# Four graph layers on one core: attention of a graph starts half a graph earlier, and the dilation holds two edge buffers instead of three

## The chip, the core and the metric

The kernel runs on one core of a Trainium2 chip. The metric is the device time in microseconds of one execution. A core has five engines with a queue each: PE (matmul), DVE (vector), ACT (activation), POOL (GpSimd) and SP, which here only issues DMAs. Each queue works strictly in its order; engines wait for each other and for DMAs by semaphores. POOL issues DMAs too: those that change the element type, and the loads of adjacency.

## What is computed

There are 16 graphs of 1024 nodes with 128 features, and four layers, each followed by a residual sum and a layer normalization:

```
x0: v, q, k = relu(x W + b); h = masked clip(q k^T); x = LN(x + softmax(h) v)
x1: p = x (W1 - W2) + b; q = x W2
    x = LN(x + max over neighbours j of relu(p_i + q_j))
x2: agg = A^T x;  x = LN(x + mask * (relu(((1+eps) x + agg) W1 + b1) W2 + b2))
x3: A' = dilate(A): for n = 0..1023 in turn: of row n, every (ceil(num/2))-th neighbour is
    removed when num > 10 (every one when 1 < num <= 10), and column n with it
    three SAGE layers on A' with normalized rows and batch norms over all graphs, a linear layer
    x = LN(x + linear)
```

The dilation depends on the adjacency alone, so it runs beside layers 0 to 2. It is sequential: what row n removes changes the rows after it.

## The kernel before

**The piece loop.** Layer 1's maximum over neighbours is done by table. The 1024 possible neighbours of a graph are cut into NP = 86 pieces of 12, each of two groups of 6. `tables_of` (its maxima are L492) builds, for sets of pieces, the maximum of q over each of the 64 subsets of a group; `table` and `low_part` turn two pieces of a set on PE and split them into a high and a low part (L848 to L858). `count` (L835, L836) makes on PE and ACT a one-hot `hot` that says which subset each node has as neighbours. `look_up` (L867) multiplies table by hot into PSUM (`pg`), and DVE takes the maximum into `best` (L932; L926 for the first piece). A piece is worked in two halves of 512 nodes; `slot(s)` writes down the work of piece s out of 16 x 86 = 1376. Two `pg` buffers exist.

**Order.** In the piece loop the order of PE, ACT, DVE and POOL is what the program writes down (`manual_schedule`); SP's order is set by the framework. Beside the pieces run generators called streams: `scores(b)` and `attend(b)` (layer 0 and the two products of layer 1 for graph b), `tables_of(b)`, and `rest(b)` (end of layer 1 and layer 2). A stream yields `ask(engine, cost, ...)` and goes on when its engine's account in `room` is positive, a delay in pieces has passed, and an event such as `("q", b)` has happened. The accounts are refilled at each half piece out of ROOM (L792; the new values are in the change). In graph b's 86 pieces the kernel also works on the attention of b+1 and on `rest(b-1)`.

**Row buffers and adjacency.** `X[b]` (three buffers) holds the node rows of a graph; SP loads it at the first piece of graph b-1. `An[b]` (two buffers) holds the adjacency rows of a graph. POOL loads them once for `scores` and once more for `rest` (L757).

**The dilation.** `dilation()` is a generator of its own that goes on when its due time in pieces has come. It works 32 rows at a time, all 16 graphs side by side: K = 32 blocks of about 43 pieces. Block k:

- DVE adds up counts and writes `rest` (L661).
- POOL runs 31 steps, one for each row but the last of the block (L675 to L685). Each step is ten small instructions that depend on each other. The program writes a step down every 1.03 pieces, and between the steps it writes down `behind`, the removal of block k-1's edges from all columns (`remove`: PE turns E and ranks the edges, DVE marks the removed), and then `prepare(k+1)`.
- `hit` goes to DRAM and comes back in another layout on SP (L692, L695).
- DVE turns it (`hit_T`, L709) and cuts E; POOL works out the block's numbers (L713 on).

`load(k)` allocates and fetches block k's edges `E` (four POOL DMAs, L518; three buffers), fetches `gone_T` (SP, L523), clears `counts` (POOL, L529) and allocates V. It is called for block k+1 at the start of block k, ahead of the first step:

```
work = [behind]
if k + 1 < K:
    following = load(k + 1)
    work.append((cost, False) for cost in prepare(k + 1, *following))
```

After the piece loop a last phase computes layer 3 (its aggregations are L1096), about 1.1 ms.

Of the kernel before, what the change touches and what calls it, by code (L numbers as in the profile page):

```python
# [29 lines left out]
F32 = mybir.dt.float32  # L30
# [17 lines left out]
NP = -(-N // PS)  # L48
TG = 12
R, G = 32, 4  # L50
GONE = 1
# [4 lines left out]
LOWEST = -(2.0**100)  # L56
MAGIC = 2.0**23
CLAMP_HI = 90000000000000.0
PENALTY = 2.0**100
# [16 lines left out]
def tile_graph_layers(ctx: ExitStack, tc, a, out):  # L76
# [168 lines left out]
    def layers_012():  # L245
# [65 lines left out]
        def scores(b):  # L311

            if b > 1:
                yield ask("Pool", 0, after=("p", b - 1))
            if b > 2:
                yield ask("Pool", 0, after=("rest", b - 3))
            load_rows(b)
            xT = w4.tile([P, N], F32, name="xT")
            yield from columns_of(xT, X[b])
            qT = w4.tile([P, N], F32, name="qT")  # L320
            yield from product_of(WqT, xT, qT, AF.Relu, bq)
            kT = w4.tile([P, N], F32, name="kT")
            yield from product_of(WkT, xT, kT, AF.Relu, bk)
            v = values[b] = w4.tile([P, T, D], F32, name="v")
            for h in range(2):
# [10 lines left out]
            for t in range(T):  # L336

                yield ask("A", 1.05)
                off = w4.tile([P, N], BF, name="off", tag="pen")
                nc.scalar.activation(off, An[b][:, t, :], AF.Identity, bias=ones[:, 0:1], scale=-1.0)  # L340
                if t > 1:
                    yield ask("PE", 0, same=True, after=("back", b, t - 2))
                e = w4.tile([P, N], F32, name="e", bufs=2)

                tops = small.tile([P, 2], F32, name="tops")
                for h, s in enumerate(halves):
                    for i in range(2):
                        yield ask("PE", 0.5 if i else 0.74, take=(i == 0), same=(i == 1))
                        if i == 0:
                            psc = shared("psc")  # L350
                            nc.tensor.matmul(psc, penalty, off[:, s], start=True, stop=False)
                        nc.tensor.matmul(psc[:, 256 * i:256 * (i + 1)], qT[:, t * P:(t + 1) * P],
                                         kT[:, s.start + 256 * i:s.start + 256 * (i + 1)], start=False, stop=(i == 1))
                    yield ask("V", 0.77, give=True)
                    nc.vector.tensor_scalar(e[:, s], psc, CLAMP_HI, None, op0=ALU.min, op1=ALU.max,
                                            accum_out=tops[:, h:h + 1])
                yield ask("V", 0.1, same=True)
                top = small.tile([P, 1], F32, name="top")
                nc.vector.tensor_scalar(top, tops[:, 0:1], tops[:, 1:2], -1.0, op0=ALU.max, op1=ALU.mult)
                yield ask("A", 1.1)  # L360
                total = small.tile([P, 1], F32, name="total")
                nc.scalar.activation(e, e, AF.Exp, bias=top, accum_out=total)
                exps[b, t] = e, total
                happened["e", b, t] = now
            yield ask("A", 0.01, after=("X1", b), delay=0.5)
            xT = w4.tile([P, N], F32, name="xT1", tag="xT")
            yield from columns_of(xT, X[b])
# [11 lines left out]
        def attend(b):  # L379
            for t in range(T):  # L380
                yield ask("PE", 0.01, after=("e", b, t))
                if t == 0:
                    y = w4.tile([P, T, D], F32, name="y0", tag="xT")
                e, total = exps.pop((b, t))
# [18 lines left out]
                nc.vector.reciprocal(share, total)  # L403
                nc.vector.scalar_tensor_tensor(y[:, t, :], pav, share, X[b][:, t, :], op0=ALU.mult, op1=ALU.add)
            yield from norm(X[b], y)
            happened["X1", b] = now
# [69 lines left out]
        def tables_of(b):  # L476

            if b:
                yield ask("V", 0, urgent=True, after=("tables", b - 1))
            for g0 in range(0, NP, TG):  # L480
                n_g = 2 * min(TG, NP - g0)
                yield ask("V", 0.01, same=True, urgent=True, after=("q", b))
# [23 lines left out]
        def dilation():  # L506
# [7 lines left out]
            def load(k):  # L514
                own = slice(k * R, (k + 1) * R)
                E = dil.tile([P, Q, N], F8, name="E", bufs=3)
                for g in range(G):
                    nc.gpsimd.dma_start(out=E[g * R:(g + 1) * R], in_=adj_q[g, own])  # L518
                gone_T = None
                if k > 2:  # L520
                    gone_T = dil.tile([P, Q, N], BF, name="gone_T")
                    for q in range(Q):
                        nc.sync.dma_start(out=gone_T[:, q, :(k - 2) * R],  # L523
                                          in_=removed_T[k, :, q, :(k - 2) * R])

                counts = dil.tile([P, 6, Q], F32, name="counts", bufs=2)
                nc.gpsimd.memset(counts, 0.0)  # L529
                V = dil.tile([B, R, R], BF, name="V", bufs=2)  # L530
                return E, V, gone_T, counts

# [45 lines left out]

            def remove(k, E, shifts, least, match):

# [11 lines left out]
                def turn(q, h, ET):  # L592
                    p = borrow("pturn")
                    for c in range(4):
                        at = slice((4 * h + c) * P, (4 * h + c + 1) * P)
                        nc.tensor.matmul(p[:, c * P:(c + 1) * P], E[:, q, at], ident_b, start=(c == 0), stop=(c == 3))
                    nc.scalar.copy(ET[:, 4 * h:4 * h + 4, :].rearrange("p c i -> p (c i)"), p)
                    given[lent] = now + 0.5

                def ranked(q, h, ET, rank):  # L600
                    p = borrow("prank")
                    for i in range(4):
# [3 lines left out]
                                         beyond[:, 512 - n:] if h else upto[:, :n], start=(i == 0), stop=(i == 3))  # L606
                    nc.scalar.activation(rank[:, halves[h]], p, AF.Abs, bias=shifts[:, h, q:q + 1])
                    given[lent] = now + 0.5

                lent = None  # L610
                ranks = [None] * Q
                for q in range(Q + 1):
# [10 lines left out]
                    if q < Q:  # L623
                        turn(q, 1, ET)
                    if q and after > 0:
                        nc.vector.transpose(last_T[:, q - 1].rearrange("p k r -> p (k r)"), gone[:, (k + 2) * R:])
# [11 lines left out]
            for _ in prepare(0, *this):  # L638
                pass
            behind = iter(())  # L640
            for k in range(K):
# [11 lines left out]
                for c, slots in enumerate(((0, 2, 3, 5), (1, 4))):  # L653
                    for i in slots:
                        nc.tensor.matmul(p[:B, c * R:(c + 1) * R], spread[:, i].rearrange("p q g -> p (q g)"), of_row,
                                         start=(i == slots[0]), stop=(i == slots[-1]))
                yield 0.5, 0.2, False
                low = dil.tile([B, R], F32, name="low_counts")
# [4 lines left out]
                yield 0.5, 0.2, k > 0  # L663
                work = [behind]
                if k + 1 < K:
                    following = load(k + 1)
                    work.append((cost, False) for cost in prepare(k + 1, *following))
                work = (what for part in work for what in part)
                gp = nc.gpsimd
# [65 lines left out]
                if k + 1 < K:  # L735
# [10 lines left out]
                    this = following  # L746
                behind = remove(k, E, shifts, least, match)
            for cost, gives in behind:
                yield 0.5, cost, gives

        def load_x(b):
            X[b] = apool.tile([P, T, D], F32, name="X", bufs=3)
            nc.sync.dma_start(out=X[b], in_=x[b].rearrange("(t p) d -> p t d", p=P))
# [28 lines left out]

        columns_in = [apool.tile([P, N], BF, name=f"AT{i}") for i in range(4)]
        for t in columns_in:
# [6 lines left out]

        ROOM = {"PE": 1.5, "A": 0.8, "V": 1.8, "Pool": 9.0}  # L792
        room = dict.fromkeys(ROOM, 0.0)

# [44 lines left out]
        def table(s):  # L839

            b, g = divmod(s, NP)
            g0 = g - g % TG
            assert ("sub", b, g0) in happened, (s, [(x.__name__, pending[x]) for x in streams], room)
            pt = psum.tile([P, 512], F32, tag="subset", name="pt", bufs=2)[:, :2 * P]
            if g + 2 - g0 == min(TG, NP - g0):
                happened["used", b, g0] = now
# [38 lines left out]
        def slot(s, last):  # L885
# [4 lines left out]
            if s >= 0 and g == 0:  # L890
                bests[b] = bests[b - 1] if b else w4.tile([P, 2, N], F32, name="best")
                if b + 1 < B:
                    start(tables_of(b + 1), True)
                    load_x(b + 1)
                    start(attend(b + 1))
                    start(scores(b + 1))
            if s >= 0 and g % PC == 0:
                load_columns(b * (T + 1) + g // PC + 2)
            for h in range(2):
                now = s + 0.5 * h  # L900
                for e in ROOM:
                    room[e] = min(room[e] + ROOM[e] / 2, ROOM[e] / (2 if e in ("PE", "V") else 1))
                if s >= 0:
                    pg = psum.tile([P, 2, 512], F32, tag="wide", name="pg", bufs=2)
                    look_up(s, h, pg)
                if h == 0 and s % 2 and s + 1 < last:
                    low_part(s + 1)
                if h and s % 2 == 0 and s + 2 < last:
                    table(s + 2)
                early = s >= 0 and due < now  # L910
                if early:
# [484 lines left out]
```

## Time and profile before

| what | before |
| --- | --- |
| device time, median of 3 runs | 6037.21 us (6033.12 to 6038.86) |
| the profiled execution | 6037.15 us |
| its span, first to last instruction | 6035.3 us |
| piece loop, first L926 to last L932 | 139 to 4922 us |
| busy in the piece loop: PE, DVE, ACT, POOL | 4408, 4251, 3202, 3482 us |
| granted TensorE clock over the span | 0.934 |

The span is what the trace shows; the 1.85 us between it and the time of the same execution lie around it. Busy shares are read by stretch: the piece loop and the last phase have different limits. Idle time is put down to what ended it. A graph in the middle of the loop takes about 300 us: from 2819.2 to 3120.7 us, graph 9's 301.5 us, PE is busy 282.9 us and DVE 269.0 us. The last graph, with no attention beside it, takes 289.2 us.

### The profile page before, as it was taken

How to read it: one execution, taken by the hardware profiler on the slowest of the kernel's cores; microseconds unless marked ns; L12 is line 12 of the kernel's file. 1: busy time of each engine (PE TensorE's matmuls, PEld its weight loads, DVE VectorE, ACT ScalarE, POOL GpSimd, SP SyncE). 2: the span in 40 equal slices, each digit the busy share in tenths (PEclk: the TensorE clock that was granted, in tenths of full speed). 3: DMA queues.
4: the chain of work that ended last, by engine and by line, in shares of the span. 5: the costliest groups of instructions: out<-in, count | busy, mean ns of one | idle time of the engine just before them, and what ended most of it. 6: DMA issues, size and time to landing. Idle time of an engine off the chain costs nothing. (4 is left out here: it accounts for less than half of the span.)

```text
span 6035.3 us, 93326 instructions
## 1 busy us (share of the span) xinstructions
PE 5505.7 (91%) x30250; PEld 3233.1 (54%) x30250; DVE 4867.4 (81%) x7488; ACT 3828.5 (63%) x7362; POOL 3706.1 (61%) x12040
## 2 busy tenths in 40 slices
PE   5989999999899999899999999999998878999998
PEld 4545555555555555555555555555554435555654
DVE  3888899899989898889888989898989855554455
ACT  3666676767666666666667666666666544444855
POOL 2676777777777777777777777777777731110124
PEclk8989998999998999899989898999898989999999
DMA  5123232323232222222222222222221135554645
GB/s 45 20 42 47 48 49 47 47 48 48 47 47 47 46 46 47 46 47 49 45 48 46 47 46 47 46 48 46 48 45 37 32 66 144 144 141 136 223 162 195
DMA packets 517791, 400.36 MB, mean 66 GB/s; under 512 B 308274, under 2 KB 435764, under 8 KB 512692
## 3 DMA queue, kind: packets, MB, share of 16 engines
q0 software_dynamic: 108000, 116.73, 17.0%
q1 hardware_dynamic: 407328, 277.07, 15.4%
q8 instruction: 237, 3.88, 0.3%
q14 instruction: 254, 2.08, 0.1%
q10 hardware_dynamic: 1972, 0.59, 0.0%
HBM read 458.57 MB, written 167.51 MB: 104 GB/s over the span
## 5 line engine op out<-in xcount | busy, mean ns | idle before, releaser
L932 DVE TENSOR_TENSOR best<-best,pg 128x1024 f32<-128x1024 f32 x2720 | 3251.6, 1213 | 414.1 <-PE pg L867 396.5
L836 ACT ACTIVATE hot<-pm 128x512 fp32r<-128x512 f32 x2752 | 1634.4, 596 | 799.8 <-PE pm L835 780.5
L867 PE MATMUL pg<-hot,high 64*128 64x512 f32 x5504 | 1736.3, 561 | 244.9 <-DVE best L932 224.6
L867 PE MATMUL pg<-hot,low 64*128 64x512 f32 x5504 | 1437.7, 416 | 0.0
L835 PE MATMUL pm<-AT,lit 61*128 61x512 bf16 x2752 | 1125.2, 409 | 84.3 <-ACT hot L836 81.6
L867 PEld LDWEIGHTS pg<-hot,high 64*128 64x128 f32 x5504 | 598.0, 199 | 539.8 <-DVE best L932 468.0
L867 PEld LDWEIGHTS pg<-hot,low 64*128 64x128 f32 x5504 | 829.3, 203 | 9.1
L835 PEld LDWEIGHTS <-lit 61*128 61x128 bf16 x2752 | 261.1, 95 | 616.5 <-issue 530.0
L675 POOL TENSOR_SCALAR sc<-low_counts,half_mask,rest 16x1 f32<-16x1 f32 x992 | 352.6, 355 | 360.3 <-DVE rest L661 234.3
L680 POOL TENSOR_SCALAR sc<-sc 16x1 f32<-16x1 f32 x992 | 394.5, 398 | 105.5
L851 ACT CAST high<-pt 128x256 fp32r<-128x256 f32 x688 | 255.9, 372 | 250.6 <-PE pt L848 245.5
L677 POOL TENSOR_SCALAR sc<-sc 16x1 f32<-16x1 f32 x992 | 324.6, 327 | 107.8
L1141 POOL TENSOR_TENSOR length<-length,mhalf 128x8 f32<-128x8 f32 x48 | 78.9, 1643 | 488.0 <-DVE length L1140 488.0
L682 POOL TENSOR_SCALAR hit<-V,sc 16x31 bf16<-16x31 bf16 (+30 forms) x992 | 361.2, 364 | 0.0
L858 ACT CAST low<-pt 128x256 fp32r<-128x256 f32 x688 | 256.1, 372 | 159.7 <-PE pt L856 156.4
L683 POOL TENSOR_SCALAR last_rank<-V,sc 16x31 f32<-16x31 bf16 (+30 forms) x992 | 344.1, 347 | 0.0
L492 DVE TENSOR_TENSOR sub<-sub,q 128x24 f32<-128x24 f32 (+11 forms) x768 | 308.0, 402 | 24.6 <-ACT q L307 10.4
L848 PE MATMUL pt<-ident,sub 128*128 128x128 f32 x1376 | 322.6, 319 | 0.2
L400 PE MATMUL pav<-v,eT 128*128 128x128 f32 x2048 | 294.8, 289 | 2.3 <-ACT eT L393 2.3
L848 PEld LDWEIGHTS pt<-ident,sub 128*128 128x128 f32 x1376 | 145.7, 148 | 276.6 <-issue 141.0
L676 POOL TENSOR_SCALAR sc<-sc 16x1 f32<-16x1 f32 x992 | 234.4, 236 | 86.6
L678 POOL TENSOR_SCALAR sc<-sc 16x1 f32<-16x1 f32 x992 | 232.5, 234 | 83.2
(272 smaller groups left out, 9990.1 us busy)
## 6 DMA issues: line engine op xcount, KB each, us to landing
removed<-gone SPq DMA_DIRECT2D x128, 256.0 KB
AT<-in_adjT_dram POOLq DMA_DIRECT2D x272, 120.0 KB, 3.1
adjb<-AT SPq DMA_DIRECT2D x272, 120.0 KB
An<-in_adj_dram POOLq DMA_DIRECT2D x31, 1024.0 KB, 14.5
E<-in_adj_dram POOLq DMA_DIRECT2D x128, 128.0 KB, 6.3
adj<-adjb POOLq DMA_DIRECT2D x16, 1024.0 KB, 8.4
gone_all<-removed POOLq DMA_DIRECT2D x64, 256.0 KB, 10.2
near<-adj SPq DMA_DIRECT2D x16, 1024.0 KB
```

What stands on the lines that cost most here:

```text
L400: nc.tensor.matmul(pav, eT[:, c, :], values[b][:, c, :], start=(c == 0), stop=(c == T - 1))
L492: nc.vector.tensor_max(sub[:, :n_g, n:2 * n], sub[:, :n_g, 0:n], qg[:, 2 * g0:2 * g0 + n_g, k:k + 1].to_broadcast([P, n_g, n]))
L675: gp.tensor_scalar(half, mine, half_mask[:, m], rest[:, n:n + 1], op0=ALU.mult, op1=ALU.add)
L677: gp.tensor_scalar(sf, half, 5.5, sf, op0=ALU.is_gt, op1=ALU.mult)
L680: gp.tensor_scalar(to, at, sf, none, op0=ALU.subtract, op1=ALU.subtract)
L682: gp.tensor_scalar(hit[:, n, n + 1:], V[:, n, n + 1:], at, None, op0=ALU.is_equal)
L683: gp.tensor_scalar(last[:, n + 1:], V[:, n, n + 1:], to, None, op0=ALU.is_le)
L835: nc.tensor.matmul(pm, lit[rows, r, :], AT[b * (T + 1) + c][rows, halves[h]], start=True, stop=True)
L836: nc.scalar.activation(hots[s][:, halves[h]], pm, AF.Relu)
L848: nc.tensor.matmul(pt[:, k * P:(k + 1) * P], subs[b, g0][:, g - g0 + k, :], ident, is_transpose=True, start=(k == 0), stop=(k == 1))
L867: nc.tensor.matmul(pg[:, a], part[rows, at * P:(at + 1) * P], hots[s][rows, halves[h]], start=(k == 0), stop=(k == 1))
L932: nc.vector.tensor_max(own, own, pg)
```

## The change

- `scores(b+2)` and `attend(b+2)` start at piece FIRST = 35 of graph b instead of at the first piece of graph b+1. Graph 1's start at the first piece of all, as before. `load_x` moves into `scores`, X has four buffers, xT two. `An[b]` is loaded when the last scores of graph b-1 are made; v of graph b waits for the end of b-1's attention.
- E has two buffers. `load(k+2)` is called in `remove(k)`, which runs in block k+1, when PE's last turn of E has been written down.
- The tables are made in eight sets of 12, 12, 10, 10, 10, 10, 10 and 12 pieces instead of seven of 12 and one of 2.
- The accounts of PE and DVE have other refills (`ROOM`, and `FULL` in the first four graphs), and `table`, `low_part` and the dilation's matmuls are now charged to PE's account.
- The four buffers of adjacency columns move from one pool to another, on the other side of memory.

```diff
+SETS = ((0, 12), (12, 12), (24, 10), (34, 10), (44, 10), (54, 10), (64, 10), (74, 12))
+SET_OF = [g0 for g0, n in SETS for _ in range(n)]
+FIRST = 35
...
         def scores(b):
-            if b > 1:
-                yield ask("Pool", 0, after=("p", b - 1))
-            if b > 2:
-                yield ask("Pool", 0, after=("rest", b - 3))
+            if b > 3:
+                yield ask("Pool", 0, after=("rest", b - 4))
+            if b:
+                load_x(b)
+                yield ask("PE", 0, delay=2.0)
+            xT = w4.tile([P, N], F32, name="xT", bufs=2)
+            yield from columns_of(xT, X[b])
+            if b:
+                yield ask("Pool", 0, after=("e", b - 1, T - 1))
             load_rows(b)
-            xT = w4.tile([P, N], F32, name="xT")
-            yield from columns_of(xT, X[b])
...
+            if b:
+                yield ask("PE", 0, after=("av", b - 1))
             v = values[b] = w4.tile([P, T, D], F32, name="v")
...
-                if t > 1:
-                    yield ask("PE", 0, same=True, after=("back", b, t - 2))
+                if t > 1 or b:
+                    yield ask("PE", 0, same=True, after=("back", b, t - 2) if t > 1 else ("back", b - 1, T + t - 2))
...
+            happened["av", b] = now
             yield from norm(X[b], y)
...
-            for g0 in range(0, NP, TG):
-                n_g = 2 * min(TG, NP - g0)
+            for g0, size in SETS:
+                n_g = 2 * size
...
-                E = dil.tile([P, Q, N], F8, name="E", bufs=3)
+                E = dil.tile([P, Q, N], F8, name="E", bufs=2)
...
                     nc.scalar.copy(ET[:, 4 * h:4 * h + 4, :].rearrange("p c i -> p (c i)"), p)
+                    room["PE"] -= 0.22
...
                     nc.scalar.activation(rank[:, halves[h]], p, AF.Abs, bias=shifts[:, h, q:q + 1])
+                    room["PE"] -= 0.54
...
                     if q < Q:
                         turn(q, 1, ET)
+                    if q == Q - 1:
+                        turned()
...
+            def load_next(k):
+                nonlocal following
+                if k < K:
+                    following = load(k)
...
-                work = [behind]
-                if k + 1 < K:
-                    following = load(k + 1)
-                    work.append((cost, False) for cost in prepare(k + 1, *following))
-                work = (what for part in work for what in part)
+                following = None
+                if k == 0:
+                    load_next(1)
+
+                def beside(k=k):
+                    yield from behind
+                    if k + 1 < K:
+                        for cost in prepare(k + 1, *following):
+                            yield cost, False
+
+                work = beside()
...
-                behind = remove(k, E, shifts, least, match)
+                behind = remove(k, E, shifts, least, match, lambda k=k: load_next(k + 2))
...
-            X[b] = apool.tile([P, T, D], F32, name="X", bufs=3)
+            X[b] = apool.tile([P, T, D], F32, name="X", bufs=4)
...
-        columns_in = [apool.tile([P, N], BF, name=f"AT{i}") for i in range(4)]
+        columns_in = [w2.tile([P, N], BF, name=f"AT{i}") for i in range(4)]
...
-        ROOM = {"PE": 1.5, "A": 0.8, "V": 1.8, "Pool": 9.0}
+        ROOM = {"PE": 1.7, "A": 1.0, "V": 1.2, "Pool": 9.0}
+        FULL = {"PE": 2.0, "A": 1.0, "V": 1.8, "Pool": 9.0}
...
-                    load_x(b + 1)
-                    start(attend(b + 1))
-                    start(scores(b + 1))
+            for at in ([1] if s == 0 else []) + ([b + 2] if s >= 0 and g == FIRST and b + 2 < B else []):
+                start(attend(at))
+                start(scores(at))
...
-                    room[e] = min(room[e] + ROOM[e] / 2, ROOM[e] / (2 if e in ("PE", "V") else 1))
+                    most = FULL[e] if s < 4 * NP else ROOM[e]
+                    room[e] = min(room[e] + most / 2, most / (2 if e in ("PE", "V") else 1))
...
                     low_part(s + 1)
+                    room["PE"] -= 0.11
...
                     table(s + 2)
+                    room["PE"] -= 0.32
```

More of the change, by code (lines that the diff above doesn't have):

```diff
@@ L365, in scores @@
             yield ask("A", 0.01, after=("X1", b), delay=0.5)
-            xT = w4.tile([P, N], F32, name="xT1", tag="xT")
+            xT = w4.tile([P, N], F32, name="xT1", tag="xT", bufs=2)
             yield from columns_of(xT, X[b])
@@ L382, in attend @@
                 if t == 0:
-                    y = w4.tile([P, T, D], F32, name="y0", tag="xT")
+                    y = w4.tile([P, T, D], F32, name="y0", tag="xT", bufs=2)
                 e, total = exps.pop((b, t))
@@ L577, in prepare, with remove @@
                     yield 0.6
-            def remove(k, E, shifts, least, match):
+            def remove(k, E, shifts, least, match, turned):
                 nonlocal last_T
@@ L639, in dilation @@
                 pass
-            behind = iter(())
+            behind, following = iter(()), None
+            def load_next(k):
+                nonlocal following
+                if k < K:
+                    following = load(k)
             for k in range(K):
@@ L656, in dilation @@
                                          start=(i == slots[0]), stop=(i == slots[-1]))
+                room["PE"] -= 0.4
                 yield 0.5, 0.2, False
@@ L841, in table @@
             b, g = divmod(s, NP)
-            g0 = g - g % TG
+            g0 = SET_OF[g]
             assert ("sub", b, g0) in happened, (s, [(x.__name__, pending[x]) for x in streams], room)
             pt = psum.tile([P, 512], F32, tag="subset", name="pt", bufs=2)[:, :2 * P]
-            if g + 2 - g0 == min(TG, NP - g0):
+            if g + 2 == NP or SET_OF[g + 2] != g0:
                 happened["used", b, g0] = now
```

## The prediction

> **What bounds the kernel now.** I read four views in this order: the page's busy shares and costliest groups, the busy table of one stretch, the waits by engine, and two short timelines around the dilation.
>
> ```profile
> PE 5505.7 (91%) x30250; PEld 3233.1 (54%) x30250; DVE 4867.4 (81%) x7488; ACT 3828.5 (63%) x7362; POOL 3706.1 (61%) x12040
> L932 DVE TENSOR_TENSOR best<-best,pg 128x1024 f32<-128x1024 f32 x2720 | 3251.6, 1213 | 414.1 <-PE pg L867 396.5
> L867 PE MATMUL pg<-hot,high 64*128 64x512 f32 x5504 | 1736.3, 561 | 244.9 <-DVE best L932 224.6
> 139.00:4922.00 4783.00, 4408.04 (x25014) 2556.10 (x25014) 4250.73 (x6213) 3201.91 (x6410) 3482.41 (x11628) 0.93 0.27 45
> ```
>
> The page's line of busy shares puts PE first, but the change touches only the piece loop, which runs from the first L926 (139 us) to the last L932 (4922 us): 4783 us for 2752 half pieces, 1.738 us each. There (last line: PE, PEld, DVE, ACT, POOL) PE is busy 92% and DVE 89%, and the two group rows show each waiting for the other: DVE 397 us for pg, PE 225 us for best. Only two pg buffers lie between them, so a half piece costs about the larger of its PE work and its DVE work. What attention, rest and dilation put into one half piece decides.
>
> The waits of DVE and POOL and two timelines show a second bound:
>
> ```profile
> DVE hit_T L709 <- DMA hit_p<-hit: 37.9, 7, 18.1
> POOL sc L675 <- DVE rest L661: 234.3, 27, 15.2
> ...
> 1750.12 1.17 POOL L772 DMA_DIRECT2D AT<-in_adjT_dram  x2 [0.29 <-issue]
> 1751.28 2.20 POOL L518 DMA_DIRECT2D E<-in_adj_dram  x4
> 1753.46 0.14 POOL L529 MEMSET counts<- 128x24 f32 x1
> 1764.12 0.32 POOL L675 TENSOR_SCALAR sc<-low_counts,half_mask,rest 16x1 f32<-16x1 f32 x1 [10.51 <-DVE rest L661]
> ...
> 1583.70 0.31 SPq L692 DMA_DIRECT2D hit<-hit  x1
> 1583.75 0.18 POOL L685 TENSOR_TENSOR low_counts<-low_counts,hit 16x1 f32<-16x1 f32 x1
> 1585.25 1.74 SPq L695 DMA_DIRECT2D hit_p<-hit  x4
> 1588.42 0.31 DVE L709 STREAM_TRANSPOSE hit_T<-hit_p 128x128 bf16<-128x128 bf16 x1 [6.63 <-DMA hit_p<-hit]
> 1590.64 0.80 PE L867 MATMUL pg<-hot,high 64*128 64x512 f32 x2 [6.96 <-DVE best L932]
> ```
>
> Each of the 32 dilation blocks runs 31 dependent steps on POOL (L675 to L685), from DVE's rest (L661) to the trip of hit through DRAM, which DVE's hit_T (L709) needs at a fixed place of its order. In block 9 (last five lines) DVE stood 6.63 us for it, and PE 6.96 us behind DVE: such a wait is lost in full. In block 11 (lines 3 to 6) POOL issues the four E loads in 2.20 us and then idles 10.51 us until rest comes: today those loads lie in idle time.
>
> **How near that chain is.** From L675's first to L685's last start and end in the POOL timeline, a chain takes 120.7 us on average: 109.8 us of its own (3.54 a step) and 10.9 us of other POOL work between the steps. hit_T can start 4.5 to 6 us later (4.75 in block 9; 11.0 at most). So rest to hit_T needs 126.0 us on average. The engines take 128.6 us over the same stretch, waits taken out. The margin is 2.6 us on average, not in each block: adding the shortfalls block by block gives 42 us; the trace has 43.4 (37.9 for hit_p, and 5.5 in one block that the view of L709 books on a neighbouring DMA). The method holds for before.
>
> **The change, part by part.**
>
> *Attention sooner, and new accounts.* These remove no matmul or maximum; they move work between pieces. I took the instruction order of both programs, cut it at each L932, and gave every instruction the mean time from its start to the next one's in this trace where nothing idled between (L932 1.135 us, L355 0.61, L492 of 768 elements 0.88, a 256-wide f32 matmul 0.27). Both orders sum to 3793 us on PE and 4098 on DVE. The sum over half pieces of the larger of the two is 4651 us before (measured 4783, 3% more) and 4604 after: 47 less. Half pieces above 2.0 us fall from 564 to 432. So the move does what it says: q of graphs 6 to 15 is made 20 to 28 pieces ahead of its graph, against 3 to 11. Split at the dilation's marks, the stretches rest to hit_T lose 52 us (53 at their measured scale of 1.017), all else gains 5. Graphs 1 to 3 get longer, 4 to 14 shorter.
>
> *Two edge buffers.* E for block k+2 cannot be loaded until remove(k) has turned E of block k. In the new order the four loads and the counts memset stand behind the 14th of the 31 steps in each of 30 blocks, no longer ahead of the first. They leave the idle time and enter the chain: 4 x 0.57 (the mean of their row) = 2.3 us a block. The Trainium skill, page "DMA: Bandwidth & Descriptors", section "Latency and other measured facts", charges a DMA issued by GpSimd about 1 us for writing its descriptors. That would be 4.0 us a block, 1.7 more, some 35 us over the blocks that are short; the row of this very load has 0.57, so I take 2.3 and keep the rule's for the high end. SP's gone_T loads keep their place ahead of hit in SP's order.
>
> *Other POOL work moved.* An loads (1.03 us each) now come one per block, and both subtractions into left (2.1 us each) fall into the same even blocks. Together with E the other work inside the chains rises from 10.9 to 14.1 us on average.
>
> *Sum for the chain.* rest to hit_T then needs 126.0 + 3.3 = 129.3 us, the engines 128.6 - 1.65 = 126.9: the mean margin turns from +2.6 to -2.4. Block by block the shortfalls add to 122 us with each block's own measured scale and 129 with the mean scale; I take 125, 82 more than the 43 now. Late next is hit_T, in about 20 blocks against 8; behind it on DVE stand the maxima, and behind those PE.
>
> *What a wait gives back.* During it PE finishes two half pieces of pg. The next two cost DVE's part alone, (4651 - 4098)/2752 = 0.2 us less each: 20 waits x 0.4 = 8; of the 8 present ones 3 are in the time before. Net -5.
>
> *Small parts.* Eight table sets of 12 or 10 instead of seven of 12 and one of 2: as many instructions and elements, no time of their own. Does E come late? prepare(k+2) begins some five steps of 1.03 pieces after the load, about 18 us; a load lands in 6.3 us (median; longest 25.2): 0, at most 7 in a rare block. Does POOL wait for the turned buffer? It reaches the place after 14 x 3.54 = 50 us plus other work, PE after 14 x 1.03 x 3.45 = 50 us: 0, at most 2 a block. An finds its buffer free in every load; X loads stand early in SP's order, behind the x3 store of an older graph. Freer spacing may shorten PE's waits for ACT (pe for e 46.7 us, pm for hot 81.6, over the whole span): between 0 and -30, I take -8, since these are the short waits of crowded pieces. The columns' buffers change sides of memory, so the last phase's first loads may wait for other tiles: -5 to +5, taken as 0.
>
> Sum: -53 + 5 + 82 - 5 - 8 = +21 us. The profiled execution took 6037.15 us (span 6035.3 and 1.85 around it), the median of the runs 6037.21: no difference. 6037 + 21 = 6058.
>
> **Rivals.**
>
> *Forecast: the chain decides (0.54).* For it: 8 waits of this kind today, the method's 42 us against 43.4 measured, and PE standing behind DVE. Likeliest 6058, own range 6045 to 6100.
>
> *Smoothing wins (0.29).* If the chain's shortfalls rise by less than about 60 us, that is, if half of the added POOL work falls where POOL waits anyway or the chain's own steps get shorter, then -53 + 5 - 5 - 8 + 30 = -31, 6006; with no new wait at all 5976. Against it: inside the chains of before no wait of POOL exceeds 3 us, so nothing hides the loads. For it: the ledger of half pieces is rough, and the measured time tracks it within 3% only over whole graphs, so that its 47 could be 80.
>
> *They cancel (0.17).* Within 12 us of now, 0.2% and about what a measurement of this kernel can tell from no change: shortfalls up by some 60 us.
>
> *Worse than forecast (within the 0.54).* E late or its buffer not free: 30 x 2 us for the buffer, or the rule's 35: 6095 to 6120. It decides if landings exceed 18 us in many blocks.
>
> *The change doesn't do what it says.* If attention stayed against its graph's start, half pieces above 2.0 us would stay near 564 and only the chain's cost remain: about +50. The order speaks against it.
>
> **How the numbers follow.** 6058 is the forecast's likeliest. The low end 5995 takes in most of the smoothing case and leaves under 0.1 below; the high end 6100 takes the unknown costs of E in part and leaves about 0.1 above. Faster 0.29, same 0.17, slower 0.54.
>
> **What would show it.** Right: hit_T waits of 100 us or more in about 20 blocks; E loads in POOL's timeline between two L675-type steps; longer idling of POOL ahead of the first step; DVE's wait for pg down from 397 us to some 350. Wrong: hit_T waits below 80 us, the own part of a chain below 109 us, or graphs 6 to 13 under 296 us each (now about 300).

## The result: 2.5% slower, and two waits that the prediction had not counted

The changed kernel took 6180.5 us (median of 4 runs, 6165.64 to 6200.94) against 6035.2 us before (4 runs): a ratio of 1.0247, interval 1.0212 to 1.0282, so some 149 us. The forecast had the direction, for a reason that is only part of it, and a size of 21 us.

The same views after the change: first the page's busy shares, its two costliest groups, and the stretch of the piece loop (columns: PE, PEld, DVE, ACT, POOL busy, clock, DMA share, GB/s):

```profile
PE 5518.5 (89%) x30250; PEld 3227.8 (52%) x30250; DVE 4857.8 (78%) x7488; ACT 3833.5 (62%) x7362; POOL 3711.4 (60%) x12040
L962 DVE TENSOR_TENSOR best<-best,pg 128x1024 f32<-128x1024 f32 x2720 | 3253.1, 1212 | 500.6 <-PE pg L894 486.6
L894 PE MATMUL pg<-hot,high 64*128 64x512 f32 x5504 | 1742.9, 561 | 280.7 <-DVE best L962 254.4
140.90:5082.70 4941.80, 4419.73 (x25018) 2550.55 (x25018) 4240.76 (x6213) 3207.29 (x6411) 3488.44 (x11629) 0.92 0.27 43
```

No engine works noticeably more in the loop: PE 4420 us against 4408, DVE 4241 against 4251. The loop is 159 us longer in this execution (the slowest of the four), nearly all of it idle time. The last phase is within 5 us of before. DVE's wait for pg did not fall from 397 us to 350; it rose to 487. The waits of DVE, PE and ACT (us in total, times, longest) say what stood in the way:

```profile
DVE square L551 <- DMA E<-in_adj_dram: 106.6, 25, 8.4
DVE hit_T L735 <- DMA hit_p<-hit: 42.2, 8, 17.4
PE pm L862 <- ACT hot L863: 130.0, 91, 17.7
PE pa L454 <- ACT parts L443: 35.1, 8, 9.1
ACT parts L443 <- POOL left L446: 129.6, 24, 14.4
```

and two lines of before that belong beside them:

```profile
PE pm L835 <- ACT hot L836: 81.6, 84, 18.5
ACT parts L434 <- POOL left L437: 18.5, 5, 10.2
```

Line 1 is new: DVE stands 25 times for E, at the head of `prepare`. Line 2 is what it was (43.4 with the one booked elsewhere): the wait on which the forecast rested did not grow. The waits of `parts` are the surprise: ACT's copies into `parts`, in the stream `rest`, stood 18.5 us for POOL's subtraction into `left` and now stand 129.6. ACT makes `hot` for every half piece, so PE's pm waits behind it (81.6 us before, 130.0 now).

Of the prediction's signs, two came: the E loads stand between two steps of the chain, and POOL idles longer ahead of its first step (306.8 us for rest in total, 234.3 before). The two that carried its sum did not: hit_T waits neither 100 us nor in 20 blocks, and its 42.2 us lie below the 80 that were named as a sign of being wrong; DVE's wait for pg did not fall.

Both waits as the timeline shows them, block 21 first: POOL issues the loads, DVE stands at square, PE behind DVE.

```profile
3442.11 2.31 POOL L527 DMA_DIRECT2D E<-in_adj_dram  x4 [0.34 <-ACT hot L863]
3450.33 0.23 DVE L551 CAST square<-E 128x128 bf16<-128x128 fp8e4 x1 [7.88 <-DMA E<-in_adj_dram]
3452.41 0.79 PE L894 MATMUL pg<-hot,high 64*128 64x512 f32 x2 [6.70 <-DVE best L962]
...
3336.33 2.11 POOL L446 TENSOR_TENSOR left<-left,parts 128x1024 f32<-128x1024 f32 x1
3338.47 1.04 ACT L443 CAST parts<-left 128x1024 bf16<-128x1024 f32 x1 [10.17 <-POOL left L446]
3339.57 0.61 PE L454 MATMUL pa<-An,parts 128*128 128x512 fp8e4 x1 [9.08 <-ACT parts L443]
3341.60 1.22 DVE L962 TENSOR_TENSOR best<-best,pg 128x1024 f32<-128x1024 f32 x1 [9.72 <-PE pg L894]
```

DVE was ready for square at 3442.45, a third of a microsecond after POOL had begun to issue the load. In the second stretch ACT stands 10.17 us, PE 9.08, DVE 9.72: one late subtraction on the least loaded engine stops the other three.

The traces show how late that subtraction is. Counted over graphs 0 to 14, each with two copies that need `left`: before, POOL had it done 9.2 us after the end of the copy that it follows, on average, and ACT was ready for the next copy after 16.0 us; POOL was the later one 3 times of 30. After the change POOL needs 14.3 us, ACT is ready after 10.9, and POOL is the later one 22 times.

### The profile page after: what moved, and what is told of

The parts are those of the page before. It is cut to its first block, busy times and chain, and to the rows that moved or that the text cites. A ratio compares the mean times of both kernels' runs of the same rounds, so it can differ in the third digit from the quotient of the medians.

```text
span 6199.2 us, 93385 instructions
## 1 busy us (share of the span) xinstructions
PE 5518.5 (89%) x30250; PEld 3227.8 (52%) x30250; DVE 4857.8 (78%) x7488; ACT 3833.5 (62%) x7362; POOL 3711.4 (60%) x12040
## 4 chain that ended last, share of the span: by engine, by line
PE 42%; POOL 28%; DVE 14%; issue 8%; ACT 5%; DMA 3%; SPq 0%; POOLq 0%; DVEq 0%; ACTq 0%
PE pg L894 9%; DVE best L962 7%; PE pm L862 5%; PE pagg L1126 5%; POOL sc L706 3%; POOL sc L701 3%; POOL hit L708 3%; POOL last_rank L709 3%; PE pa L454 3%; POOL sc L703 2%; PE pav L408 2%; POOL sc L702 2%; POOL hit L710 2%; POOL low_counts L711 2%; POOL sc L704 2%
## 5 line engine op out<-in xcount | busy, mean ns | idle before, releaser
L701 POOL TENSOR_SCALAR sc<-low_counts,half_mask,rest 16x1 f32<-16x1 f32 x992 | 355.8, 359 | 443.9 <-DVE rest L681 306.8
L706 POOL TENSOR_SCALAR sc<-sc 16x1 f32<-16x1 f32 x992 | 393.6, 397 | 105.4
L703 POOL TENSOR_SCALAR sc<-sc 16x1 f32<-16x1 f32 x992 | 319.1, 322 | 107.8
L501 DVE TENSOR_TENSOR sub<-sub,q 128x160 f32<-128x160 f32 (+11 forms) x768 | 306.8, 401 | 23.5 <-ACT q L310 10.3
L360 PE MATMUL psc<-kT,qT 128*128 128x256 f32 x1024 | 303.4, 395 | 0.0
L408 PEld LDWEIGHTS pav<-v,eT 128*128 128x128 f32 x2048 | 265.1, 200 | 49.9 <-issue 24.6
```

Of the source, the lines that this page charges most:

```text
L408: nc.tensor.matmul(pav, eT[:, c, :], values[b][:, c, :], start=(c == 0), stop=(c == T - 1))
L701: gp.tensor_scalar(half, mine, half_mask[:, m], rest[:, n:n + 1], op0=ALU.mult, op1=ALU.add)
L703: gp.tensor_scalar(sf, half, 5.5, sf, op0=ALU.is_gt, op1=ALU.mult)
L706: gp.tensor_scalar(to, at, sf, none, op0=ALU.subtract, op1=ALU.subtract)
```

## The experiments

Each ratio is to the runs of the kernel before on the same chip.

**Is E's lateness lost in full, and what does the wait for left cost?** Three edits of the changed kernel and one of the kernel before. `late_prepare` lets three steps pass ahead of prepare:

```diff
                     yield from behind
+                    if k:
+                        for _ in range(3):
+                            yield 0, False
```

> The changed kernel, with three empty steps ahead of prepare(k+1), so that E is first read three steps (some 3.1 pieces, 10.8 us) later; nothing else. Theory A (E arrives late because POOL reaches the loads late, and each wait of DVE is lost nearly in full): DVE's wait of square for E falls from 106.6 us to under 10, hit_T's wait stays under 80, and the time falls by 75 to 115 us, to about 6085. Theory B (the POOL chain bounds the block, as the prediction had it; the wait for E only stands where the wait for hit_T would): hit_T's wait rises from 42 us to over 100 and the time falls by less than 40 us. Theory C (the moved attention costs, not the dilation): less than 30 us, with DVE's wait for pg still near 487 us.

Ratio 1.0221 (1.0206 to 1.0236); the changed kernel had 1.0247. E's wait fell as meant, and almost nothing came of it:

```profile
DVE square L551 <- DMA E<-in_adj_dram: 5.6, 3, 2.2
DVE hit_T L738 <- DMA hit_p<-hit: 54.0, 9, 17.0
PE pm L865 <- ACT hot L866: 189.4, 93, 19.8
ACT parts L443 <- POOL left L446: 155.4, 20, 20.8
```

101 us less at square; 12 more at hit_T, 26 more at parts, 59 more at pm. The ratios differ by 16 us and their intervals overlap, so a gain is not even shown. Theory A fails here, and so does B: the wait did not return at hit_T but at ACT. C's forecast of the time (under 30 us) is met, but DVE's wait for pg is 527.5 us, above C's 487; the next run shows what it stands behind. A reading that fits, though no run shows it alone: while DVE stands for E the other engines stand too and POOL catches up; take that wait away, and POOL is as late for the next one who needs it.

`left_delay` spaces the copies into parts:

```diff
-                yield ask("A", 1.05, delay=2.5 if k else 0.5)
+                yield ask("A", 1.05, delay=6.0 if k else 0.5)
```

> The changed kernel, with the second and third copy into parts asked for 6.0 pieces after the one before instead of 2.5, so that POOL has the subtraction into left done before ACT needs it; nothing else. Theory A with its second part (ACT stands for left because POOL runs behind the written order, and hot, and so PE, stand behind ACT): ACT's wait of parts for left falls from 129.6 us to under 30, PE's wait of pm for hot from 130 to about 85, and the time falls by 60 to 110 us, to about 6095. Theory B and C: the wait goes, but the time falls by less than 30 us, because DVE waits for hit_T or pg instead.

Ratio 1.0075 (1.006 to 1.009): some 104 us gained, the largest single effect, as the second part of theory A had it. Parts and pm wait about as before the change; E's wait fell too, and hit_T's rose:

```profile
ACT parts L443 <- POOL left L446: 21.7, 8, 4.8
PE pm L862 <- ACT hot L863: 82.6, 91, 10.2
DVE square L551 <- DMA E<-in_adj_dram: 44.6, 17, 7.8
DVE hit_T L735 <- DMA hit_p<-hit: 63.2, 17, 10.3
```

`late_and_delay` has both edits:

> The changed kernel with both edits: three empty steps ahead of prepare, and 6.0 pieces between the copies into parts. Theory A: both gains add to 140 to 210 us, so that what is left is the smoothing of the half pieces: 5975 to 6040, ratio to before 0.99 to 1.00. Theory B: hit_T's waits come up to 120 us, 6060 to 6090. Theory C: above 6100, DVE's wait for pg near 480.

Ratio 1.0037 (1.0025 to 1.0049), with no wait for E left (0.2 us):

```profile
DVE best L965 <- PE pg L897: 412.2, 621, 13.4
DVE hit_T L738 <- DMA hit_p<-hit: 72.4, 16, 8.7
ACT parts L443 <- POOL left L446: 27.4, 7, 10.8
```

This is between A and B: with the two unforeseen waits gone, the kernel is 22 us slower than before. This is the case that the prediction had priced, and hit_T is among what it stands for: 76.7 us with the 4.3 booked on a neighbouring DMA, in 17 blocks. That 22 lies so near the forecast's 21 is in part luck, as the sum below shows. Late E costs 0.38% (left_delay to here), about 23 us.

`before_two_edges` is the kernel before with two E buffers and load(k+2) in remove(k), nothing else:

> The kernel before with the dilation part of the change alone: two E buffers and load(k+2) in remove(k); attention, sets, accounts and column buffers as before. Theory A: square waits 50 to 110 us for E, the time rises by 50 to 110 us, to about 6115. Theory B: the waits stand at hit_T (90 us or more), the time rises by 20 to 60. Theory C: less than 15 us.

Ratio 1.0086 (1.0069 to 1.0102): 52 us, with square waiting 25.6 us and hit_T 61.8 (52.4, and 9.4 booked elsewhere). C is out: the dilation's part costs with the old attention too. The time fits A and B alike, but the waits are below what either asked for.

**Which part brings the copies too close?** `three_edges_delay` is the changed kernel with the dilation's buffers as before and the wider copies. The room comes from two other tiles:

```diff
-                E = dil.tile([P, Q, N], F8, name="E", bufs=2)
+                E = dil.tile([P, Q, N], F8, name="E", bufs=3)
...
-                        rank = ranks[q] = dil.tile([P, N], F16, name="rank", bufs=2)
+                        rank = ranks[q] = dil.tile([P, N], F16, name="rank", bufs=1)
...
-                        gone = dil.tile([P, N], BF, name="gone", bufs=2)
+                        gone = dil.tile([P, N], BF, name="gone", bufs=1)
...
-                if k == 0:
-                    load_next(1)
+                load_next(k + 1)
...
-                behind = remove(k, E, shifts, least, match, lambda k=k: load_next(k + 2))
+                behind = remove(k, E, shifts, least, match, lambda: None)
```

> The changed kernel with the dilation's buffers as before (three for E, load(k+1) ahead of the first step of block k) and 6.0 pieces between the copies into parts. For room, rank and gone of remove have one buffer instead of two. What is left of the change is the sooner attention, the accounts and the even sets. Theory S (the smoothing of half pieces that the prediction priced at 47 us is real and was hidden by the two POOL waits): no wait for E, parts waits under 30 us, hit_T 30 to 60, DVE's wait for pg under 400; 5980 to 6005 us, ratio 0.991 to 0.996. Rival (the ledger of half pieces promises what the engines do not give): 6020 to 6045.

Ratio 0.9955 (0.994 to 0.997): 27 us below before, the fastest so far. The gain is about half of what was priced. The time from the first to the last maximum's start is 4761 us in its profile, 4781 before, and hit_T waited as before:

```profile
DVE best L961 <- PE pg L893: 406.6, 624, 11.3
PE pg L893 <- DVE best L961: 190.2, 327, 3.4
DVE hit_T L734 <- DMA hit_p<-hit: 41.2, 13, 8.3
ACT parts L443 <- POOL left L446: 16.7, 5, 5.0
```

Theory S holds but for one sign: DVE's wait for pg did not fall below 400 us. What fell is the other side, PE's wait for best, from 224.6 to 190.2. The intervals between successive maxima (by their starts) that exceed 2.0 us went from 689 before to 608; the prediction's ledger had 132 fewer. Graphs 0 to 3 took 22 us longer in this profile and graphs 4 to 15 took 42 us less. Parts wait no less than before to speak of (18.5 there), so the wider copies are hardly what gained.

`three_edges` is the same with the copies at 2.5 pieces:

> As three_edges_delay, but the copies into parts asked for 2.5 pieces apart, as in the changed kernel. Theory P (the copies come too close together because ACT's account is larger, whatever the E loads do): parts wait 70 to 140 us for left, and the time is 40 to 100 us above three_edges_delay. Rival (the copies wait because the E loads hold POOL up): parts wait under 45 us, and the time is within 20 us of three_edges_delay.

Ratio 1.0143 (1.0126 to 1.016), 113 us above its neighbour, more than theory P had set:

```profile
PE pm L861 <- ACT hot L862: 165.6, 102, 21.1
ACT parts L443 <- POOL left L446: 151.3, 25, 16.6
```

The rival is out: the copies are too early without any load inside the chain. Whether ACT's account is why, as P says, the next run asks.

`before_account` changes one number in the kernel before:

```diff
-        ROOM = {"PE": 1.5, "A": 0.8, "V": 1.8, "Pool": 9.0}
+        ROOM = {"PE": 1.5, "A": 1.0, "V": 1.8, "Pool": 9.0}
```

> The kernel before with ACT's account refilled by 1.0 instead of 0.8, alone. Theory P: the copies into parts come 3 pieces apart instead of 5.5, parts wait 60 to 130 us for left instead of 18, and the time rises by 30 to 90 us. Rival (only the moved attention or the E loads bring the copies ahead of POOL): parts under 40 us, the time within 15.

Ratio 0.9999 (0.9989 to 1.0009). Going by the `hot` instructions between two copies in the traces, 23 of 30 copies lie 5.5 pieces after the one before in the kernel before; with this account 15 lie 5.0 pieces apart and 12 lie 3 to 4.5; in the changed kernel 19 lie 3.0 apart. Parts waited 40.9 us, and the time stayed. So P fails: ACT's account alone is not the cause. Something else of the change belongs to it, and which part was not tried. The sooner attention may leave ACT's account full when `rest` asks, but no run shows this.

`before_one_rank`, the control for the buffers:

> A control for the two runs with three edge buffers: the kernel before with one buffer for rank and for gone. By every theory the time stays within 12 us (0.2%) of before; if it rises, that much of the two runs' time is due to these buffers.

Ratio 0.9997 (0.9988 to 1.0005): nothing.

**Is it the wait itself, or where `rest` stands?** `copies_of_x` leaves every instruction in place and takes the dependence away:

```diff
-                nc.scalar.copy(parts[:, k], left if k else X[b])
+                nc.scalar.copy(parts[:, k], X[b])
```

> The changed kernel with all three copies into parts made from X instead of the second and third from left. Every instruction stays in its place, POOL's subtractions too, but ACT no longer waits for them; the split of X into three parts is thereby left out (its two smaller parts are wrong), so it is no version to use. Theory P (the wait of ACT for POOL's left is what costs, not the spacing of the copies): parts wait for left 0, and the time falls by 80 to 115 us to about 6085, as in left_delay. Rival (the later and wider placing of rest in left_delay made the gain): less than 40 us.

Ratio 1.0093 (1.0072 to 1.0114), 93 us less than the changed kernel. In the two profiles the instructions of DVE, ACT and POOL stand in the same order, so nothing was moved: the wait is the cause. The bill moved once more in part, to hit_T:

```profile
DVE best L962 <- PE pg L894: 354.2, 600, 10.3
DVE square L551 <- DMA E<-in_adj_dram: 106.0, 24, 8.6
DVE hit_T L735 <- DMA hit_p<-hit: 72.7, 17, 15.3
PE pm L862 <- ACT hot L863: 81.1, 84, 15.6
```

DVE's wait for pg is 354.2 us here, near the 350 that the prediction had named as a sign, but not for its reason: in three_edges_delay, which has the smoothing and no wait for E, it is 406.6. Here DVE stands 106 us at square, in which time PE can get ahead. PE's pm waits as before the change.

**The price of the loads inside the chain, apart from E's lateness.** `before_two_late` is before_two_edges with the three empty steps:

> before_two_edges with three empty steps ahead of prepare(k+1), so that E has landed when it is read. Theory A (E's wait is lost nearly in full): square waits under 3 us and the time falls by 20 to 30 us against before_two_edges, to a ratio of 1.004 to 1.006. Theory B (the chain on POOL bounds the block): hit_T waits rise from 52 us to 75 or more and the time falls by less than 12 us, ratio 1.007 to 1.010.

Ratio 1.006 (1.0038 to 1.0082), against 1.0086 with E late; the intervals overlap. No wait for E remains; hit_T waits 47.7 us, less than B asked for, and parts 40.1. So E's lateness costs some 16 us in this kernel, with that width.

`before_loads_in_chain` keeps three E buffers and puts the four loads behind the 14th step, one block sooner than they are needed. They stand in a function of their own, `load_edges`, which is called for the first three blocks ahead of the loop:

```diff
...
-            def remove(k, E, shifts, least, match):
+            def remove(k, E, shifts, least, match, turned):
...
+                    if q == Q - 1:
+                        turned()
...
-                behind = remove(k, E, shifts, least, match)
+                behind = remove(k, E, shifts, least, match, lambda k=k: load_edges(k + 3))
```

> The kernel before with three E buffers, but the four loads of E made inside the chain, behind the 14th step, for the block after the next, so that E can never be late: the loads' price in the chain alone. By the sum of the prediction (2.3 us more in each of 29 chains against the margins of before): hit_T waits 75 to 95 us instead of 43, time +30 to +45 us, ratio 1.005 to 1.0075. Rival (a longer chain finds slack that the margins do not show): hit_T under 55, ratio under 1.002.

Ratio 1.006 (1.0039 to 1.0082), 36 us:

```profile
DVE hit_T L719 <- DMA hit_p<-hit: 63.9, 13, 16.8
DVE hit_T L719 <- DMA adjb<-AT: 8.9, 1, 8.9
```

hit_T waits 72.8 us together, 29 more than before, where at least 75 was expected; the time is as expected. From rest to the end of POOL's last step takes 123.1 us on average, 120.7 before: 2.4 more, where four issues of 0.57 us make 2.3. So the prediction's way of costing the chain (what the loads add, against each block's margin) holds for the thing that it was made for.

**A middle spacing.** `three_edges_delay4` has 4.5 pieces between the copies:

> three_edges_delay with 4.5 pieces between the copies instead of 6.0. Theory P: parts wait 30 to 70 us for left and the time lies 10 to 50 us above three_edges_delay. Rival: 4.5 pieces are enough and rest's earlier end makes it the best version, 5995 to 6010.

Ratio 0.9991 (0.9978 to 1.0003), some 22 us above three_edges_delay as the ratios have it; parts waited 29.8. That is theory P at its low edge, and the rival is out. three_edges_delay remains the best version that was run.

## Why the prediction was wrong

Put end to end, the runs give the change in four parts (ratio of the run, and what it adds to the row above, in us of 6035):

| step | ratio | adds |
| --- | --- | --- |
| sooner attention, accounts, sets, columns' buffers (three_edges_delay) | 0.9955 | -27 us |
| loads of E inside the chain (late_and_delay) | 1.0037 | +49 us |
| E late (left_delay) | 1.0075 | +23 us |
| copies into parts wait for POOL (the change) | 1.0247 | +104 us |

From the intervals of the ratios, the first three parts are good to some 10 us and the last to some 25 (an estimate). The second part also holds the three empty steps of late_and_delay; with the old attention the loads cost 36 us without these steps (before_loads_in_chain) and with them (before_two_late). The order of taking away matters little to the last part: it is 111 us without late E (late_prepare to late_and_delay) and 113 with no loads in the chain (three_edges).

Going by the profiles and step by step:

- **Attention sooner: right in kind, too large.** -48 us were worked out from the ledger and -8 for freer waits; -27 (interval -36 to -18) came. The ledger takes each half piece for itself; why it promised too much was not tried.
- **The loads in the chain: the mechanism was right, the size too large.** The chain grew as worked out: from rest to the end of POOL's last step it takes 124.1 us on average after the change, 120.7 before, 3.4 more where 3.3 was set. But hit_T was to wait 125 us, and 77 net of what a wait gives back was to be paid. With the other two waits gone hit_T waits 76.7 us, and the loads cost 49; 36 on the old order. So late_and_delay comes to +22 where the forecast had +21, from two errors of some 28 us each that cancel. In the changed kernel the loads' cost cannot be seen at hit_T, which waited 42.2 us. DVE comes to hit_T 133.6 us after rest there, 128.6 before, so the margin may have come back because other waits had slowed the block. This is argued, not shown: in three_edges the same copies wait, and hit_T waits 80.7 us.
- **"Does E come late? ... 0": the first step that failed.** It set a landing of 6.3 us against 18 us between two places of the written order. But POOL does not keep pace with the written order, it runs behind it. The profile of the change has, on average over 30 blocks and from rest: PE's last turn of E ended at 45.3 us, the loads issued at 55.8, E landed at 64.9, DVE ready for square at 61.9. From issue to reader there were 6.1 us, not 18, and the landing of all four took 9.1, not 6.3. The numbers were at hand: 50 us of steps, half of the 10.9 us of other work, 2.3 of issue and 6.3 of landing make 64; 18.5 pieces of 3.45 us make 64. The margin was nothing, and the trace of before has DVE at square 65.7 us after rest. The prediction did compare POOL with PE for the buffer, and rightly called that wait small; for the data it forgot POOL's delay. With the old attention DVE is ready only after 65.6 us (before_two_edges), and E's wait is 25.6 us instead of 106.6. The 30 blocks' late E costs some 23 us.
- **What was not in the sum: the step that failed by most, 104 us.** "Other POOL work moved" counted what moved into the chain and asked only who stands behind it on POOL. It did not ask who on other engines waits for it. The subtractions into left were named, with 2.1 us each and the remark that both now fall into the same blocks; their reader, ACT's copy, was not. The program holds ACT's copy back by a stated delay of 2.5 pieces, 8.7 us; before, ACT's account stretched that to 5.5 pieces in 23 of 30 cases, and the change let it shrink to 3 in 19. So ACT asks after 10.9 us instead of 16.0, and POOL, which has steps of 3.5 us ahead of the subtraction, is done after 14.3 instead of 9.2. Both sides moved; why POOL came later too was not separated.
- **The rivals.** "Worse than forecast" named late E, at 6095 to 6120, as decided by landings over 18 us; late E came with landings of 9.1 us from the first issue, because of POOL's place. The smoothing case's own part was real at half its size, and stood behind three waits on POOL's work.
- **What POOL would hold for an issue.** The sum took 0.57 us a load and kept 1 us for the high end; the loads took 0.57 us (median) in the changed kernel too, so that part of the high end was not called on.
- **"Such a wait is lost in full"** was right for the block that it was read from, and misleading for sums. Taking 101 us of E's wait away brought 16 us or nothing (late_prepare); taking left's 129.6 us away brought 93 us, and hit_T 30 us more of waiting (copies_of_x); 22 us more of left's wait cost nothing that the runs can tell (before_account). We read the three waits as one lateness of POOL that meets whoever asks first. What the runs show is that the lengths of these waits do not add up to time.

## What to carry to other kernels

When one engine runs behind the order in which the program is written, a distance in that order is no distance in time. List every reader of that engine, on all engines and in DMAs, and compare two times from one common event: when it will have finished, and when the reader will ask. When a change shifts load accounts or buffer counts, look for delays that had been kept by accident: here a tight account had spaced copies that the stated delay alone leaves too close together. And after removing a wait, look where its engine is late next before counting the gain.

## What had not been expected of the hardware

Four loads of 128 KB issued one after the other by POOL land 9.1 us after the first issue on average over 30 blocks of the changed kernel, though the profile's page gives a median of 5.9 us from one issue to its landing: for the set, the issue time (4 x 0.57 us) comes on top, and the slowest of the four counts. And an engine busy 60% of the span, POOL, could stop all of the others: its chain takes 3.5 us for a step of ten instructions, and in the stretch at 3336 us the end of one subtraction of 2.11 us ended 10.17 us of standing of ACT and, behind ACT, 9.08 us of PE and 9.72 us of DVE.
